# Fewer adjacency pieces per slot and fewer small VectorE operations in the first step of a graph layer

## The chip, the core and the metric

The kernel runs on one core of a Trainium2 chip. The metric is the device time of one execution in microseconds (us). The engines are called as in the profile: PE (TensorE, matrix products), DVE (VectorE), ACT (ScalarE), POOL (GpSimd) and SP (SyncE, which here only issues DMAs). [...]

## What is computed

A graph layer over N = 3327 nodes with 256 features, in two steps. In each step every node attends to all others, but only the largest probabilities that together reach 0.9 are kept. Beside it, features diffuse over a sparse adjacency matrix (about 0.12% of its entries are nonzero, and the diagonal).

```python
h = relu(layernorm(x))
R = adj + eye(N);  R = R / R.sum(-1, keepdims=True)
Z = 0;  Xf = Xa = h
for n in range(2):
    logits = (Xa @ W1.T @ W2.T) @ (Xa @ W3.T).T
    A = softmax(logits), only the top-p part (p = 0.9) kept, rows scaled to sum 1
    Xf = R @ Xf
    Xa = A @ Xa
    Z = Z + Xf @ U1[n].T + Xa @ U2[n].T
out = x + layernorm(h + Z) * g + b
```

## The kernel before

The nodes are cut into NT = 26 tiles of P = 128 rows (NP = 3328). The step loop runs over `step` 0 and 1, and inside it `i` from -1 to 27; one pass of the inner loop is called a slot here. In slot i of step 0 work on several tiles is interleaved, each piece of work being a Python generator that is advanced one stage at a time:

- `weights` (L582) makes the exponentials `e` of tile i+3. `project` (L516) makes the queries and, from `mq`, the statistics `ms` of a row's logits.
- `measured_once` (L635) guesses a row's threshold for tile i+1: two passes of ACT over the row (`through`, L633) and small operations on columns of `g`, on ACT, POOL and DVE.
- `settle` (L725) settles the exact threshold of tile i. Its stages on DVE: a pass over the row that keeps what is below the guess (`w`, L731) and `need` (L732); 20 MAX8 over segments (L736); five rounds of MAX8 and MATCH_REPLACE8 on the candidates; a running sum; the mask pass over `e` (L765); `cum` (L767) and its maximum (L769), which goes to `rec`. The final proof `prove` (L773) reads `rec`.
- `Sums` (L797) transposes the masked `e` on PE (`pt`, L810), copies it back on ACT (`eT`, L812), and multiplies with the features (`pa`, L824).
- `listed` (L837) reads the adjacency matrix. For a tile it takes 128 rows in pieces, one DMA and one DVE reduction (L846) each, and turns the block maxima into a list of the nonzero places in every row. The first nine tiles (`HALVES`) have two pieces of 13 blocks, the others seven pieces of four blocks (the last of two), in two buffers. At the end of a tile come about eight short DVE operations (L849 to L857): `lists`, four direct indices (`index`, L855) and `over`, the number of further entries.
- `packed` (L862) and `gathered` (L875) pack the further entries of a tile by small matmuls (`pb`, `po`), and `gathered` then issues the indirect DMAs on POOL: rows of the adjacency (`ac`, L894) and of the products (`xg`, L903). `diffuse` multiplies them (`pr`, L911), two slots later, in `spread`.
- `products` (L982) makes the products with U1 in the warm-up.

The order on the engines is written out by hand. `PLAN[0]` has seven strings for the seven parts of a slot of step 0; each letter advances one generator: m `measured`, d `settle`, s `spread`, a `listed`, e `first_end`, w and q `weights`, p `packed`, g `gathered`. After the seven parts the letters of a last string run what is left. The text's order is kept on PE, ACT and DVE in both steps; POOL's queue in step 0 and SP's are ordered by the scheduler.

```python
PLAN = (("mdsssa", "mdsssa", "edawwp", "msda", "mpdea", "gdawwq", "emdgq"),
c=work["d"],
a=lister if step == 0 and i else none,
for c in "lcnwqsepgb" if step else "dmwqsepgb":
```

So six pieces are read in a slot, none in slot 0. Thirteen advances of `listed` stand before slot -1, in the warm-up.

Of the kernel before, what the change touches and what calls it, by code (L numbers as in the profile page):

```python
# [9 lines left out]
F32 = mybir.dt.float32  # L10
# [3 lines left out]
AF = mybir.ActivationFunctionType  # L14
ALU = mybir.AluOpType
# [3 lines left out]
P = 128  # L19
N = 3327  # L20
D = 256
DA = 64
NT = (N + P - 1) // P
NP = NT * P
# [320 lines left out]
def guess_graph_layer(ctx, tc, x, adj, w1t, w2t, w3t, u1t, u2t, ln_g, ln_b, out, flag):  # L345
# [89 lines left out]
    back = const.tile([P, NT], F32, tag="back", name="back")  # L435
    G.iota(back, pattern=[[-1, NT]], base=NONE, channel_multiplier=-NT, allow_small_or_imprecise_dtypes=True)
    lists = const.tile([P, NT, LIST + 1], F32, tag="lists", name="lists")
    ends = const.tile([P, NT], F32, tag="ends", name="ends")
    over = const.tile([P, NT], F32, tag="over", name="over")
    index = const.tile([P, NT, DIRECT + 1], I32, tag="index", name="index")  # L440
    ax = dram.tile([NT, P, D], F32, tag="ax", name="ax")
# [74 lines left out]
    def project(step, t, queries=True, law=True):  # L516

        qp = query_at(t)
        pq = ps_t.tile([P, 4, P], F32, tag="pt", name="pq")
        pm = pq[:, 1:3, :].rearrange("p a b -> p (a b)")[:, : 2 * DA + 2]  # L520
        qT = ms = None
        if queries:
            PE.matmul(pq[:, 0, :], w2d[qp, :], query_of(t), start=True, stop=True)
        if law:
            PE.matmul(pm, query_of(t), qm[qp, step, :], start=True, stop=True)
        if queries:
            qT = tpool.tile([P, P], F32, tag="qT", name="qT", bufs=3)
            S.copy(qT, pq[:, 0, :])  # L528
        if not law:
            return qT, ms  # L530
        mq = small.tile([P, 2 * DA + 2], F32, tag="mq", name="mq", bufs=2)
        S.copy(mq, pm)
        yield


        ms = small.tile([P, 9], F32, tag="ms", name="ms")
        col = lambda k: ms[:, k : k + 1]
        V.tensor_copy(col(0), mq[:, DA : DA + 1])  # L538
        V.scalar_tensor_tensor(mq[:, : DA + 1], mq[:, : DA + 1], 1.0, mq[:, DA + 1 :], ALU.mult, ALU.mult,
                               accum_out=col(1))  # L540
        m = col(0)
        G.tensor_tensor(col(2), col(1), half[:, 1:2], ALU.pow)
        G.tensor_scalar(ms[:, 3:7], of_s, col(2), 1.0e-4, ALU.mult, ALU.add)
        G.tensor_scalar(col(7), col(1), 0.5, m, ALU.mult, ALU.add)
        G.tensor_scalar(col(7), col(7), 0.25, LNY - 0.25 * math.log(0.1 / N), ALU.mult, ALU.add)
        G.tensor_scalar(col(8), col(1), m, col(4), ALU.add, ALU.add)
        return qT, col


# [81 lines left out]
    def through(e, f, guess, sign, total):  # L631
        ja = scan.tile([P, NP], U8, tag="ja", name="ja")
        S.activation(ja, e, f, bias=guess, scale=sign, accum_out=total)  # L633

    def measured_once(r):  # L635
        e, ms = r["e"], r["ms"]


        col = guessed(r, small.tile([P, 17], F32, tag="g", name="g"))
        S.activation(col(4), col(2), AF.Square, bias=con(4))  # L640
        S.activation(col(11), col(4), AF.Identity, scale=ms(5), bias=ms(6))
        S.activation(col(1), col(0), AF.Exp, scale=-1.0, bias=con(5))
        G.tensor_scalar(col(7), col(9), -0.5, None, ALU.mult)
        G.tensor_scalar(col(8), col(9), 0.5 * NP, None, ALU.mult)
        G.tensor_scalar(col(12), col(9), -1.0, None, ALU.mult)
        G.tensor_scalar(col(5), col(1), OFFSET[0], None, ALU.mult)
        G.tensor_scalar(col(10), col(9), col(5), 1.0, ALU.mult, ALU.add)
        yield
        oa = small.tile([P, 3], F32, tag="oa", name="oa")
        through(e, AF.Relu, col(9), -1.0, oa[:, 0:1])  # L650
        yield
        through(e, AF.Sign, col(12), 1.0, oa[:, 1:2])
        yield
        S.activation(col(3), oa[:, 0:1], AF.Identity, scale=-1.0, bias=col(8))
        S.activation(col(4), oa[:, 1:2], AF.Relu, scale=col(7), bias=col(3))
        S.activation(col(6), col(4), AF.Ln, scale=col(1), bias=con(2))
        S.activation(col(3), col(4), AF.Square, scale=col(1), bias=con(1))
        S.activation(col(3), col(3), AF.Ln, scale=0.5, bias=col(10))
        S.activation(col(3), col(3), AF.Identity, scale=-1.0, bias=col(6))
        S.activation(col(3), col(3), AF.Exp, scale=col(11))  # L660
        yield

        V.tensor_scalar(col(5), oa[:, 1:2], 31.0 - NP, BIG, ALU.is_lt, ALU.mult)
        V.tensor_scalar(col(6), col(4), col(1), 0.35, ALU.mult, ALU.is_lt)
        V.scalar_tensor_tensor(col(5), col(6), BIG, col(5), ALU.mult, ALU.add)
        V.tensor_scalar(col(3), col(3), 1.0e20, col(9), ALU.min, ALU.mult)
        V.tensor_tensor(col(16), col(3), col(5), ALU.add)
# [57 lines left out]
    def settle(step, t, r):  # L725
# [38 lines left out]
        else:  # L764
            V.scalar_tensor_tensor(e, e, at(1), e, ALU.is_ge, ALU.mult, accum_out=ra)  # L765
        V.reciprocal(ra, ra)
        (G if step else V).tensor_tensor(cum[:, :n], dr[:, :n], b, ALU.mult)  # L767
        yield
        V.tensor_reduce(at(2), cum[:, :n], AX.X, ALU.max)  # L769

    def prove(step):  # L773
        v8, t, tn, Z = (rec[:, step, k, :] for k in range(4))
        ok = small.tile([P, NT], F32, tag="cum", name="ok", bufs=1)
        o2 = small.tile([P, NT], F32, tag="dr", name="o2", bufs=1)
        V.tensor_tensor(ok, v8, t, ALU.is_lt)
        V.tensor_tensor(o2, tn, t, ALU.is_lt)
        V.tensor_tensor(ok, ok, o2, ALU.mult)
        for a, c, op in ((tn, 0.0, ALU.is_gt), (t, 0.5 * BIG, ALU.is_lt),  # L780
                         (Z, 1.0e-30, ALU.is_gt), (Z, BIG, ALU.is_lt)):
            V.scalar_tensor_tensor(ok, a, c, ok, op, ALU.mult)
        V.tensor_scalar(ok, ok, 0.5, None, ALU.is_lt)
        n = N - (NT - 1) * P
        f = small.tile([P, 1], F32, tag="f", name="f")
        V.tensor_reduce(f, ok[:, : NT - 1], AX.X, ALU.add)
        V.tensor_tensor(fl, fl, f, ALU.add)
        V.tensor_tensor(fl[:n], fl[:n], ok[:n, NT - 1 :], ALU.add)
        if step == 0:
            V.tensor_scalar(ok, lists[:, :, LIST - 1], 0.0, None, ALU.is_gt)  # L790
            V.scalar_tensor_tensor(ok, ends, float(P), ok, ALU.is_gt, ALU.add)
            V.tensor_reduce(f, ok, AX.X, ALU.add)
            V.tensor_tensor(fl, fl, f, ALU.add)

# [42 lines left out]
    def listed():  # L837
        for t in range(NT):
# [13 lines left out]
            V.max(ls[:, :8], fm)  # L852
            V.match_replace(fm, ls[:, :8], fm, 0.0)
            V.max(ls[:, 8:LIST], fm)
            V.tensor_scalar(index[:, t, :DIRECT], ls[:, :DIRECT], -1.0, float(NONE), ALU.mult, ALU.add)  # L855
            of = small.tile([P, LIST], F32, tag="of", name="of", bufs=2)
            V.tensor_scalar(of[:, DIRECT:], ls[:, DIRECT:LIST], 0.0, None, ALU.is_gt, ALU.add,  # L857
                            accum_out=over[:, t : t + 1])
# [3 lines left out]
    def packed(t):  # L862

        assert t in done
        ls, end, ov = lists[:, t, :], ends[:, t : t + 1], over[:, t : t + 1]
        pb = ps_t.tile([P, 4, P], F32, tag="pt", name="pb")
        PE.matmul(pb[:, 0, :1], upto, ov, start=True, stop=True)
        S.copy(ls[:, LIST:], pb[:, 0, :1])
        yield
        V.tensor_tensor(end, ls[:, LIST:], ov, ALU.add)  # L870
        ohs[t] = oh = small.tile([P, P], F32, tag="oh", name="oh", bufs=2)
        V.tensor_scalar(oh, place, end, None, ALU.is_lt)
        V.scalar_tensor_tensor(oh, place, ls[:, LIST:], oh, ALU.is_ge, ALU.mult)

    def gathered(t):  # L875
# [1 line left out]
        ls, n = lists[:, t, :], LIST - DIRECT  # L877
        po = ps_t.tile([P, 4, P], F32, tag="pt", name="po")
        PE.matmul(po[:, 0, : n + 1], oh, ls[:, DIRECT:], start=True, stop=True)
        lo = small.tile([P, n + 1], F32, tag="lo", name="lo", bufs=2)  # L880
        S.copy(lo, po[:, 0, : n + 1])
        yield
        nth = small.tile([P, 1], F32, tag="nth", name="nth")
        V.tensor_scalar(nth, lo[:, n:], -1.0, part, ALU.mult, ALU.add)
        of = small.tile([P, LIST], F32, tag="of", name="of", bufs=2)
        V.scalar_tensor_tensor(of[:, :n], place[:, :n], nth, lo[:, :n], ALU.is_equal, ALU.mult, accum_out=nth)
        V.tensor_scalar(index[:, t, DIRECT:], nth, -1.0, float(NONE), ALU.mult, ALU.add)
        ac = adjp.tile([P, KT, P], F32, tag="ac", name="ac", bufs=2)
        nc.sync.dma_start(ac[:, KT - 1, :], adj[t, :, t, :])
        acs[t] = ac  # L890
# [201 lines left out]
    def refetch(t):  # L1092
# [7 lines left out]

    PLAN = (("mdsssa", "mdsssa", "edawwp", "msda", "mpdea", "gdawwq", "emdgq"),
            ("llcmss", "lnms", "lwwnfd", "lcmdsssg", "fmswqdf", "llmdf", "lmwfd"))

    LAST = {NT - 1: ("cfss", "cn", "ndd", "sss", "fddddsf", "f", "f"), NT: ("cf", "", "", "", "ff", "fv", "f"),
# [6 lines left out]
    for step in range(2):  # L1113
        sums = Sums(step, live, xw if step else x0, AHEAD[step])

        for i in range(-1, NT + 2):
# [4 lines left out]
            if step == 1 and i == -1:  # L1121
# [9 lines left out]
                s=spread(step, i - 2 + 2 * step) if valid(i - 2 + 2 * step) else none,  # L1131
                w=later.pop((step, i + 2), none),
                e=first_end(i - 2) if step == 0 and valid(i - 2) else none,
                a=lister if step == 0 and i else none,
                p=packed(i + 1) if step == 0 and i >= 0 and valid(i + 1) else none,
                g=none if not valid(i + 2 * step) else refetch(i + 2) if step else gathered(i),
                b=none, q=none, v=proof() if step and i == NT else work.get("v", none),
# [34 lines left out]
                run(work["m"])  # L1172
            if step == 0 and i == -1:
                G.memset(es[2][:, N:NP], 0.0)
            for c in "lcnwqsepgb" if step else "dmwqsepgb":
                run(work[c])
            if step == 0 and i == NT:
                moments(1, gsum)
# [52 lines left out]
```

## Time and profile before

| | |
|---|---|
| median of three runs | 1406.87 us (1405.7 to 1407.31) |
| profiled execution, device time | 1408.79 us |
| its span, first to last instruction | 1407.1 us |
| granted TensorE clock | 0.974 |
| PE busy | 1278.7 us, 91% |
| DVE busy | 1220.4 us, 87% |
| ACT busy | 1105.6 us, 79% |
| POOL busy | 989.7 us, 70% |
| first and last `need` (L732) of step 0 | 94.1 and 710.3 us |
| first `need` of step 1 | 790.8 us |
| last piece of the adjacency (L846) | 605.8 us |

Durations of single instructions are in microseconds in the timeline (start, duration) and in nanoseconds in the groups. On DVE an instruction can start a little before the end recorded for the one ahead of it, so the distance from start to start tells better what it occupies. A line of waits reads: engine, tile and line of the waiting instruction, `<-` what released it, then the sum of the idle time, how often, and the longest. A POOL instruction that is held up shows it as a longer duration, not as a wait.

### The profile page before, as it was taken

To read this page: it belongs to the slowest core of one execution; us is meant where nothing else is said; L and a number is where in the kernel's file an instruction comes from. 1 tells how busy PE (TensorE), PEld (TensorE's weight loads), DVE (VectorE), ACT (ScalarE), POOL (GpSimd) and SP (SyncE) were. 2 spreads that over 40 slices of the span, in tenths; PEclk is the share of its full clock that TensorE was granted. 3 is DMA by queue.
4 is the path that set the end of the run, shared out by engine and by line. 5 is a ranking of instruction groups with operands and counts; after the bars stand their busy time and mean duration, and the time that the engine had idled before them with its cause. 6 is when DMAs were issued, how large, how long until landed. Compare 5 with 4: busy or idle time off the path is not lost.

```text
span 1407.1 us, 22248 instructions
## 1 busy us (share of the span) xinstructions
PE 1278.7 (91%) x6495; PEld 980.9 (70%) x6495; DVE 1220.4 (87%) x3727; ACT 1105.6 (79%) x2423; POOL 989.7 (70%) x1348
## 2 busy tenths in 40 slices
PE   6898999999999999999999479999999999999885
PEld 5545777777777777778786257777777777777664
DVE  6868999999999999998863589999999999999981
ACT  5467887788778788787944689999999999999921
POOL 6214777667667677768862668888888888888832
PEclk9999999999999999999999579999999999999998
DMA  8874454544545445432331202213121221312100
GB/s 284 263 247 126 134 151 133 138 137 135 146 124 148 133 137 152 129 96 73 101 85 57 78 23 79 79 57 90 55 82 58 79 82 54 90 57 79 57 8 22
DMA packets 91203, 149.78 MB, mean 106 GB/s; under 512 B 15265, under 2 KB 58656, under 8 KB 91072
## 3 DMA queue, kind: packets, MB, share of 16 engines
q1 hardware_dynamic: 73616, 105.37, 24.0%
q0 software_dynamic: 16640, 42.69, 12.1%
q8 instruction: 54, 0.88, 0.3%
q14 instruction: 77, 0.63, 0.1%
q10 hardware_dynamic: 816, 0.20, 0.1%
HBM read 120.93 MB, written 27.28 MB: 105 GB/s over the span
## 4 chain that ended last, share of the span: by engine, by line
DVE 51%; PE 24%; ACT 17%; POOL 3%; issue 3%; DMA 1%; DVEq 0%; SPq 0%; POOLq 0%; ACTq 0%
ACT ja L633 11%; DVE e L765 10%; PE pa L824 9%; DVE cand L736 7%; DVE w L731 6%; DVE fm L846 5%; PE pl L600 4%; DVE bb L743 4%; DVE cand L745 4%; PE pt L810 3%; PE pz L988 2%; DVE x L765 2%; ACT eT L812 2%; PE pr L911 1%; ACT e L604 1%
## 5 line engine op out<-in xcount | busy, mean ns | idle before, releaser
L824 PE MATMUL pa<-xw,eT 128*128 128x256 f32 x1352 | 331.9, 387 | 6.6 <-DVE s L935 6.5
L633 ACT ACTIVATE ja<-e,g 128x3328 uint8<-128x3328 f32 x106 | 325.8, 3074 | 0.1
L824 PE MATMUL pa<-x,eT 128*128 128x256 f32 x1352 | 325.2, 382 | 0.0
L824 PEld LDWEIGHTS pa<-xw,eT 128*128 128x128 f32 x1352 | 250.2, 191 | 68.1 <-issue 27.1
L824 PEld LDWEIGHTS pa<-x,eT 128*128 128x128 f32 x1352 | 245.0, 192 | 26.3
L812 ACT COPY eT<-pt 128x512 f32<-128x512 f32 (+1 forms) x364 | 202.1, 556 | 76.6 <-PE pt L810 76.5
L736 DVE MAX8 cand<-w 128x8 f32<-128x168 f32 (+1 forms) x1040 | 251.3, 318 | 0.0
L810 PE MATMUL pt<-ident,e 128*128 128x128 f32 x1144 | 180.7, 278 | 60.6 <-DVE e L765 36.6
L894 POOL DMA_INDIRECT ac<-in_adj,index x130 | 130.7, 1005 | 128.2 <-DVE ms L538 91.2
L810 PEld LDWEIGHTS pt<-ident,e 128*128 128x128 f32 x1144 | 140.7, 144 | 107.3 <-issue 48.1
L903 POOL DMA_INDIRECT xg<-bx,index x130 | 184.8, 1421 | 41.0 <-issue 30.0
L731 DVE SCALAR_TENSOR_TENSOR w<-e,g 128x3328 f32<-128x3328 f32 x44 | 169.1, 3842 | 0.7
L903 POOL DMA_INDIRECT xg<-vx,index x130 | 131.1, 1009 | 45.6 <-issue 33.0
L765 DVE SCALAR_TENSOR_TENSOR e<-e,rec 128x3328 f32<-128x3328 f32 x40 | 156.6, 3915 | 0.7
L911 PE MATMUL pr<-xg,ac 128*128 128x257 f32 (+1 forms) x520 | 139.1, 391 | 11.5 <-DVE s L1086 11.3
L604 ACT ACTIVATE e<-pl 128x832 f32<-128x832 f32 x132 | 113.0, 859 | 36.4 <-PE pl L600 36.3
L911 PEld LDWEIGHTS pr<-xg,ac 128*128 128x128 f32 x520 | 93.9, 195 | 25.1 <-DVE s L1086 11.4
L743 DVE MAX8 bb<-cand 128x8 f32<-128x160 f32 x286 | 92.8, 325 | 6.4
L600 PE MATMUL pl<-after,qT 64*128 64x416 f32 x416 | 96.7, 559 | 0.5 <-ACT qT L528 0.5
L767 POOL TENSOR_TENSOR cum<-dr,bb 128x48 f32<-128x48 f32 x26 | 84.9, 3264 | 15.5 <-DVE rec L755 15.3
L951 POOL TENSOR_TENSOR s<-s,gam 128x256 f32<-128x256 f32 x25 | 92.5, 3701 | 3.2 <-ACT s L950 3.2
L600 PE MATMUL pl<-both,qT 64*128 64x416 f32 x416 | 90.8, 540 | 0.9 <-DVE both L1006 0.9
(259 smaller groups left out, 2210.7 us busy)
## 6 DMA issues: line engine op xcount, KB each, us to landing
at<-in_adj SPq DMA_DIRECT2D x102, 256.0 KB
cx<-ac SPq DMA_DIRECT2D x26, 384.0 KB
ac<-cx SPq DMA_DIRECT2D x26, 384.0 KB
wide<-in_adj SPq DMA_DIRECT2D x10, 832.0 KB
e<-in_adj SPq DMA_DIRECT2D x8, 832.0 KB
bx<-e SPq DMA_DIRECT2D x26, 128.5 KB
own<-bx SPq DMA_DIRECT2D x26, 128.5 KB
x<-in_x SPq DMA_DIRECT2D x13, 256.0 KB
```

The lines of the kernel that those rows point to most:

```text
L600: PE.matmul(pl[:, a, :wd], qT[p, :], keys_of(step, a).rearrange("p a b -> p (a b)")[:, c : c + wd], start=True, stop=True)
L633: S.activation(ja, e, f, bias=guess, scale=sign, accum_out=total)
L731: V.scalar_tensor_tensor(w, e, col(16), e, ALU.is_lt, ALU.mult, accum_out=d2)
L736: V.max(cand[:, 8 * s : 8 * s + 8], w[:, s * SEG : min(NP, (s + 1) * SEG)])
L743: V.max(b8, cand)
L765: V.scalar_tensor_tensor(e, e, at(1), e, ALU.is_ge, ALU.mult, accum_out=ra)
L810: PE.transpose(pt[:, j, :], e[:, (j0 + j) * P : (j0 + j + 1) * P], ident)
L812: S.copy(eT[:, :w, :], pt[:, :w, :])
L824: PE.matmul(self.pa, eT[:, c - 4 * k, :], self.xa[:, j, :], start=c == 0, stop=c == NT - 1)
L894: G.indirect_dma_start(out=ac[:, k, :], out_offset=None, in_=rows, in_offset=bass.IndirectOffsetOnAxis(ap=index[:, t, k : k + 1], axis=0), ...
L903: G.indirect_dma_start(out=xg[:, k, :w], out_offset=None, in_=rows, in_offset=bass.IndirectOffsetOnAxis(ap=index[:, t, k : k + 1], axis=0))
L911: PE.matmul(pr[:, :w], ac[:, k, :], own if k == KT - 1 else xg[:, k, :w], start=k == 0, stop=k == KT - 1)
```

## The change

In step 0 the letter a is taken out of the sixth part of `PLAN[0]`, which leaves five pieces in a slot; slot 0, which had none, takes three. The last d moves to the second part of the next slot as c. Small operations are dropped or put on another engine:

```diff
-        V.tensor_copy(col(0), mq[:, DA : DA + 1])
...
-        m = col(0)
+        minus = mq[:, 2 * DA + 1 :]
-        G.tensor_scalar(col(7), col(1), 0.5, m, ALU.mult, ALU.add)
+        G.tensor_scalar(col(7), col(1), 0.5, minus, ALU.mult, ALU.subtract)
...
-        G.tensor_scalar(col(12), col(9), -1.0, None, ALU.mult)
...
-        through(e, AF.Sign, col(12), 1.0, oa[:, 1:2])
+        through(e, AF.Sign, col(9), -1.0, oa[:, 1:2])
...
-        (G if step else V).tensor_tensor(cum[:, :n], dr[:, :n], b, ALU.mult)
-        yield
+        if step:
+            G.tensor_tensor(cum[:, :n], dr[:, :n], b, ALU.mult)
+        yield
+        if not step:
+            V.tensor_tensor(cum[:, :n], dr[:, :n], b, ALU.mult)
         V.tensor_reduce(at(2), cum[:, :n], AX.X, ALU.max)
...
-            V.tensor_scalar(index[:, t, :DIRECT], ls[:, :DIRECT], -1.0, float(NONE), ALU.mult, ALU.add)
+            G.tensor_scalar(index[:, t, :DIRECT], ls[:, :DIRECT], -1.0, float(NONE), ALU.mult, ALU.add)
...
-        V.tensor_tensor(end, ls[:, LIST:], ov, ALU.add)
-        V.tensor_scalar(oh, place, end, None, ALU.is_lt)
+        V.tensor_scalar(oh, place, ov, ls[:, LIST:], ALU.subtract, ALU.is_lt)
...
-        yield
         nth = small.tile([P, 1], F32, tag="nth", name="nth")
-        V.tensor_scalar(nth, lo[:, n:], -1.0, part, ALU.mult, ALU.add)
+        S.activation(nth, po[:, 0, n : n + 1], AF.Identity, scale=-1.0, bias=part)
+        yield
...
-        V.tensor_scalar(index[:, t, DIRECT:], nth, -1.0, float(NONE), ALU.mult, ALU.add)
+        G.tensor_scalar(index[:, t, DIRECT:], nth, -1.0, float(NONE), ALU.mult, ALU.add)
...
-    PLAN = (("mdsssa", "mdsssa", "edawwp", "msda", "mpdea", "gdawwq", "emdgq"),
+    PLAN = (("mdsssa", "mcdsssa", "edawwp", "msda", "mpdea", "gdwwq", "emgq"),
...
-                a=lister if step == 0 and i else none,
+                a=itertools.islice(lister, 9 if i else 3) if step == 0 else none,
...
-            for c in "lcnwqsepgb" if step else "dmwqsepgb":
+            for c in "lcnwqsepgb" if step else "cmwqsepgb":
```

The tile `ends` is gone; `prove` adds its two parts once, at the start of step 1. The sign of the second measuring pass turns, and with it the signs of two constants that are used with it. In the changed kernel the two index operations on POOL stand at L856 and L887, and the mask pass at L762.

More of the change, by code (lines that the diff above doesn't have):

```diff
@@ L437, in guess_graph_layer @@
     lists = const.tile([P, NT, LIST + 1], F32, tag="lists", name="lists")
-    ends = const.tile([P, NT], F32, tag="ends", name="ends")
     over = const.tile([P, NT], F32, tag="over", name="over")
@@ L537, in project @@
         col = lambda k: ms[:, k : k + 1]
-        V.tensor_copy(col(0), mq[:, DA : DA + 1])
         V.scalar_tensor_tensor(mq[:, : DA + 1], mq[:, : DA + 1], 1.0, mq[:, DA + 1 :], ALU.mult, ALU.mult,
                                accum_out=col(1))
-        m = col(0)
+        minus = mq[:, 2 * DA + 1 :]
         G.tensor_tensor(col(2), col(1), half[:, 1:2], ALU.pow)
         G.tensor_scalar(ms[:, 3:7], of_s, col(2), 1.0e-4, ALU.mult, ALU.add)
-        G.tensor_scalar(col(7), col(1), 0.5, m, ALU.mult, ALU.add)
+        G.tensor_scalar(col(7), col(1), 0.5, minus, ALU.mult, ALU.subtract)
         G.tensor_scalar(col(7), col(7), 0.25, LNY - 0.25 * math.log(0.1 / N), ALU.mult, ALU.add)
-        G.tensor_scalar(col(8), col(1), m, col(4), ALU.add, ALU.add)
+        G.tensor_scalar(col(8), col(1), minus, col(4), ALU.subtract, ALU.add)
         return qT, col
@@ L642, in measured_once @@
         S.activation(col(1), col(0), AF.Exp, scale=-1.0, bias=con(5))
-        G.tensor_scalar(col(7), col(9), -0.5, None, ALU.mult)
+        G.tensor_scalar(col(7), col(9), 0.5, None, ALU.mult)
         G.tensor_scalar(col(8), col(9), 0.5 * NP, None, ALU.mult)
-        G.tensor_scalar(col(12), col(9), -1.0, None, ALU.mult)
         G.tensor_scalar(col(5), col(1), OFFSET[0], None, ALU.mult)
@@ L661, in measured_once @@
         yield
-        V.tensor_scalar(col(5), oa[:, 1:2], 31.0 - NP, BIG, ALU.is_lt, ALU.mult)
+        V.tensor_scalar(col(5), oa[:, 1:2], NP - 31.0, BIG, ALU.is_gt, ALU.mult)
         V.tensor_scalar(col(6), col(4), col(1), 0.35, ALU.mult, ALU.is_lt)
@@ L790, in prove @@
             V.tensor_scalar(ok, lists[:, :, LIST - 1], 0.0, None, ALU.is_gt)
-            V.scalar_tensor_tensor(ok, ends, float(P), ok, ALU.is_gt, ALU.add)
+            V.tensor_tensor(o2, lists[:, :, LIST], over, ALU.add)
+            V.scalar_tensor_tensor(ok, o2, float(P), ok, ALU.is_gt, ALU.add)
             V.tensor_reduce(f, ok, AX.X, ALU.add)
@@ L864, in packed @@
         assert t in done
-        ls, end, ov = lists[:, t, :], ends[:, t : t + 1], over[:, t : t + 1]
+        ls, ov = lists[:, t, :], over[:, t : t + 1]
         pb = ps_t.tile([P, 4, P], F32, tag="pt", name="pb")
@@ L879, in gathered @@
         PE.matmul(po[:, 0, : n + 1], oh, ls[:, DIRECT:], start=True, stop=True)
-        lo = small.tile([P, n + 1], F32, tag="lo", name="lo", bufs=2)
-        S.copy(lo, po[:, 0, : n + 1])
+        lo = small.tile([P, n], F32, tag="lo", name="lo", bufs=2)
+        S.copy(lo, po[:, 0, :n])
+        nth = small.tile([P, 1], F32, tag="nth", name="nth")
+        S.activation(nth, po[:, 0, n : n + 1], AF.Identity, scale=-1.0, bias=part)
         yield
-        nth = small.tile([P, 1], F32, tag="nth", name="nth")
-        V.tensor_scalar(nth, lo[:, n:], -1.0, part, ALU.mult, ALU.add)
         of = small.tile([P, LIST], F32, tag="of", name="of", bufs=2)
-        V.scalar_tensor_tensor(of[:, :n], place[:, :n], nth, lo[:, :n], ALU.is_equal, ALU.mult, accum_out=nth)
-        V.tensor_scalar(index[:, t, DIRECT:], nth, -1.0, float(NONE), ALU.mult, ALU.add)
+        V.scalar_tensor_tensor(of[:, :n], place[:, :n], nth, lo, ALU.is_equal, ALU.mult, accum_out=nth)
+        G.tensor_scalar(index[:, t, DIRECT:], nth, -1.0, float(NONE), ALU.mult, ALU.add)
         ac = adjp.tile([P, KT, P], F32, tag="ac", name="ac", bufs=2)
```

## The prediction

> **What bounds the kernel now.** I read the engine shares first, then cut the span into stages, since a share over 1407 us mixes two steps. Only step 0 (about 94 to 790 us) is touched. Two windows of two slots each (a slot is one tile of 128 rows), first while lists are made, then after the last list piece (at 605.8 us):
>
> ```profile
> core 0: us, PE busy (x) PEld busy (x) DVE busy (x) ACT busy (x) POOL busy (x), PEclk, DMA share, GB/s
> 459.40:508.80 49.40, 47.80 (x256) 37.87 (x256) 47.60 (x155) 40.26 (x99) 34.71 (x45) 1.00 0.50 138
> 634.50:682.10 47.60, 47.60 (x257) 37.80 (x255) 41.16 (x133) 40.25 (x99) 41.07 (x45) 1.00 0.30 83
> ```
>
> TensorE is full in the second window and idles 1.6 us in the first, VectorE the other way round. The waits of 159.3 to 634.5 us (19 slots) say who holds whom:
>
> ```profile
> POOL ac L894 <- DVE ms L538: 66.6, 19, 6.4
> ...
> PE pt L810 <- DVE e L765: 17.5, 14, 2.0
> ```
>
> No VectorE wait stands in that answer: VectorE never rests, and TensorE waits 17.5 us for its masked tile (L765). From 634.5 to 705.2 the list of TensorE's waits is empty. So VectorE sets the slots with lists and TensorE those without. VectorE's slot, from `need` (L732) to `need`, with a list finished in it and without:
>
> ```profile
> 220.40 0.22 DVE L732 TENSOR_SCALAR need<-rec,d 128x1 f32<-128x1 f32 x1
> ...
> 245.56 0.21 DVE L732 TENSOR_SCALAR need<-rec,d 128x1 f32<-128x1 f32 x1
> ...
> 321.59 0.21 DVE L732 TENSOR_SCALAR need<-rec,d 128x1 f32<-128x1 f32 x1
> ...
> 345.54 0.21 DVE L732 TENSOR_SCALAR need<-rec,d 128x1 f32<-128x1 f32 x1
> ```
>
> 25.16 and 23.95 us. TensorE's own slot, where it never idles:
>
> ```profile
> 634.50 0.29 PE L879 MATMUL po<-lists,oh 128*128 128x13 f32 x2
> ...
> 657.85 0.29 PE L879 MATMUL po<-lists,oh 128*128 128x13 f32 x2
> ...
> 682.05 0.29 PE L879 MATMUL po<-lists,oh 128*128 128x13 f32 x2
> ```
>
> 23.35 and 24.20 us (tiles in COUNTED have six more matmuls), mean 23.78. That is the next floor.
>
> [...] POOL's L894 usually lasts 0.95 us and one that falls into the mask pass (L765) 4.39:
>
> ```profile
> 677.85 3.68 DVE L765 SCALAR_TENSOR_TENSOR e<-e,rec 128x3328 f32<-128x3328 f32 x1
> ...
> 677.96 4.39 POOL L894 DMA_INDIRECT ac<-in_adj,index  x1 [0.30 <-issue]
> ```
>
> [...] ops on one column still take 0.08 to 0.24 us from start to start, so dropping them is worth that.
>
> **The change part by part, per slot.** Starts of successive VectorE instructions give what each really occupies:
>
> ```profile
> 215.76 0.20 DVE L884 TENSOR_SCALAR nth<-lo,part 128x1 f32<-128x1 f32 x1
> 216.00 0.23 DVE L886 SCALAR_TENSOR_TENSOR of<-place,nth,lo 128x12 f32<-128x12 f32 x1
> 216.16 0.08 DVE L886 DVE_READ_ACCUMULATOR of<-place,nth,lo 128x1 f32 x1
> 216.27 0.15 DVE L887 TENSOR_SCALAR index<-nth 128x1 int32<-128x1 f32 x1
> 216.35 0.14 DVE L538 COPY ms<-mq 128x1 f32<-128x1 f32 x1
> 216.52 0.23 DVE L539 SCALAR_TENSOR_TENSOR mq<-mq 128x65 f32<-128x65 f32 x1
> ```
>
> - Dropped from VectorE: L884 0.24, L887 0.08, L538 0.17; `ends` (L870, 231.50 to 231.68) 0.18; sum 0.67. The direct index (L855, 227.78 to 227.90) 0.12 where a list ends.
> - One piece fewer (L846, 220.53 to 221.12): 0.59.
> - `cum` and its maximum (L767, L769) move to the next slot's second part. They took 0.44 + 0.10; behind each other they have to wait for one another, about 0.4. Bounds -0.3 to +0.1; I take nothing. Only the final proof reads them.
> - So a slot that ends a list falls from 25.16 to 25.16 - 0.59 - 0.12 - 0.67 = 23.78, another from 23.95 to 22.69. A list has seven pieces, so five of seven slots end one: mean 23.47.
> - The 119 small pieces are redistributed: none in slot 0 and six in each of 1 to 19 (four in 20) become three in slot 0, five in 1 to 23 and one in 24. Slots 21 to 23 rise from no pieces to 23.47 on VectorE, still under TensorE's 23.78. In slot 0 VectorE waits 0.25, 2.46, 1.41 and 1.64 us for `pz` or its DMA, which covers three pieces (1.8 us); the one piece taken out of the slot before it (89.00 to 89.60) pays for the first. I take 0.3 us gained in the warm-up, bounds -1 to +2.
> - ScalarE gets `nth` as an activation from PSUM (nearest row L881, 0.17; at most 0.3): it has about 20 us of work in a 23.8 us slot and `nth` is read some 7 us later. Cost nothing; without that slack 0.3 a slot.
> - POOL gets two index ops and loses L645. Like L644 to L645 (0.27 start to start) and L543 to L545 (0.35): 0.27 + 5/7 x 0.35 - 0.28 = +0.24. In its queue L887 stands ahead of the fifth row gather, the `ms` and `g` ops and later gathers. L856 waits for VectorE's list, but stands behind work that reaches it at about the time the list is done. The SP queue issues the same DMAs, one piece less per slot.
>
> Sum: 159.3 to 634.5 is 475.2 us for 19 slots. TensorE's floor is 10 x 24.20 + 9 x 23.35 = 452.2, so 23.0 can go: the 17.5 of waits [...]. I keep 1.9 us of slot 257.8 to 285.8, which is neither floor nor wait (granted clock 0.94), and 0.1 us in each of 22 slots (2.2), because slots at 23.78 on VectorE meet odd TensorE slots of 23.35; some 4 us of slack between `mq` and the next mask pass even this out. 23.0 - 1.9 - 2.2 + 0.3 = 19.2. Step 1 and the passage to it don't change. Against the profiled execution (1408.79 us, span 1407.1) this makes 1389.6; the median of the runs is 1.9 lower: **1387.7**.
>
> **Rivals.**
> - A, 0.57: TensorE's floor decides, as above. 1383 to 1392.
> - B, 0.27: [...] With POOL closer to full, VectorE's two long passes start behind a POOL op; the `w` pass at 661.73 took 4.14 instead of 3.68. If both cost 0.46 more, VectorE's mean is 24.4: (25.01 - 24.4) x 19 = 11.6, less (24.4 - 23.78) x 3 = 1.9 in slots 21 to 23: 9.7 gained, 1397. For it: step 1's passes do take 4.1. Against: those of step 0 mostly take 3.7.
> - C, 0.05: VectorE and TensorE overlap perfectly, the slow-clock stretch goes too and the warm-up gives 2 us: 25 gained, 1382.
> - D, 0.07: slower. POOL becomes the bound. Without waits its slot is already 23.93 us (L894 at 666.61 and 690.54), with the two ops 24.2. The index op is released just as pass `w` starts; [...] it loses the 1.25 us in which the gather now slips in (216.70 to 217.97): 25.4. The `g` columns then come late for ScalarE. (25.4 - 25.01) x 19 + (25.4 - 23.78) x 3 = 12: 1419. It decides once POOL needs over 25.0. Against: at 24.2, 0.4 over TensorE, the lag grows by about 9 us in 22 slots, while POOL's waits (3.5 a slot) and ScalarE's reading of the columns (L654 at 678.72, POOL done at 672.4) leave about 10.
> - E, 0.04: these cancel, within 0.2%.
>
> **How the numbers follow.** A is the likeliest, so 1387.7. Eight in ten: from 1383, leaving out half of C, to B's 1397, leaving out D and E. Faster by over 0.2% (2.8 us, about what a measurement of this kernel can tell from no change): A, B, C, 0.89; same 0.04; slower 0.07.
>
> **What would show it.** After: TensorE's waits for L762 (the old L765) nearly gone between 160 and 630 us, slots alternating near 24.2 and 23.4 to slot 23, small idle times of VectorE on `lists` and `mq`, the last piece in slot 24, and step 1 slots as before at 22.2 us. Wrong if VectorE still shows no wait and slots of 24.4 (B), if ScalarE waits for POOL's columns (D), or if slot 0 or the start of step 1 has grown.

## The result and the profile after

| | before | after |
|---|---|---|
| median of the comparison | 1406.28 us (1405.21 to 1407.31) | 1386.59 us (1383.37 to 1387.66) |
| ratio, 95% interval | | 0.9856 [0.9843, 0.9869] |
| profiled execution, its span | 1408.79, 1407.1 us | 1383.37, 1381.4 us |
| `po` (L879) of slot 2 | 159.3 us | 155.5 us |
| from there, 19 slots | 475.2 us | 455.7 us |
| the rest of the span | 772.6 us | 770.2 us |

The forecast was 1387.7 us. Of one later run, the second of less VectorE, 10 of 21 executions fell into a slower state and are left out of its median and ratio here. The profiled execution of after is the fastest of its four runs and that of before lies 2.5 us over its median, so the 25.7 us between the two spans are 6 more than the 19.7 between the medians: 3.8 lie ahead of slot 2, 19.5 in the 19 slots, 2.4 behind them.

The same two views as before, first the busy times: two slots with lists, then two later ones. In the old kernel the second window had no pieces left; now it still holds seven.

```profile
core 0: us, PE busy (x) PEld busy (x) DVE busy (x) ACT busy (x) POOL busy (x), PEclk, DMA share, GB/s
443.00:490.90 47.90, 47.81 (x255) 37.86 (x254) 44.94 (x138) 40.47 (x101) 39.25 (x48) 1.00 0.48 138
634.50:682.60 48.10, 47.53 (x254) 37.61 (x253) 45.98 (x138) 40.35 (x100) 39.83 (x43) 1.00 0.40 110
```

In the window with lists TensorE idles 0.1 us where it idled 1.6, and VectorE is busy 44.94 of 47.90 us where it was busy 47.60 of 49.40. The same view of all 19 slots, before and after:

```profile
159.30:634.50 475.20, 457.03 (x2417) 360.50 (x2417) 457.99 (x1451) 382.65 (x933) 346.53 (x427) 1.00 0.48 134
155.50:611.20 455.70, 453.93 (x2419) 359.49 (x2417) 434.90 (x1330) 385.25 (x952) 374.61 (x443) 1.00 0.47 135
```

TensorE's idle time falls from 18.2 to 1.8 us: that is 16.4 of the 19.5 us. The waits of TensorE, VectorE and POOL between 155.5 and 611.2 us, the same 19 slots:

```profile
PE pt L811 <- DVE e L762: 1.5, 4, 0.5
...
DVE fm L847 <- DMA at<-in_adj: 5.2, 10, 1.0
...
POOL ac L894 <- POOL index L887: 9.7, 19, 0.5
POOL index L887 <- DVE of L886: 8.2, 18, 0.6
```

TensorE's 17.5 us behind the mask pass have become 1.5. VectorE, which had no wait at all, now waits 5.2 us, all of it for the transfer of a piece. POOL's 66.6 us of waiting have become 17.9 in two lines. TensorE's slots from `po` to `po`:

```profile
467.48 0.29 PE L879 MATMUL po<-lists,oh 128*128 128x13 f32 x2
490.92 0.29 PE L879 MATMUL po<-lists,oh 128*128 128x13 f32 x2
...
611.16 0.29 PE L879 MATMUL po<-lists,oh 128*128 128x13 f32 x2
634.51 0.29 PE L879 MATMUL po<-lists,oh 128*128 128x13 f32 x2
659.47 0.29 PE L879 MATMUL po<-lists,oh 128*128 128x13 f32 x2
682.59 0.29 PE L879 MATMUL po<-lists,oh 128*128 128x13 f32 x2
```

23.44 and 23.35 us are TensorE's floor for a tile outside COUNTED (23.35). 24.96 is one inside COUNTED, 0.76 over its floor of 24.20: TensorE waits 0.6 us for the mask there. The last, 23.12, is as long as the same slot before (23.13). Over the 19 slots the sum stands 3.5 us above the floor of 452.2.

POOL is where the new cost went. One slot, VectorE's weight pass and what POOL does meanwhile:

```profile
473.56 3.69 DVE L728 SCALAR_TENSOR_TENSOR w<-e,g 128x3328 f32<-128x3328 f32 x1
473.58 0.19 POOL L887 TENSOR_SCALAR index<-nth 128x1 int32<-128x1 f32 x1 [0.62 <-DVE of L886]
474.28 3.83 POOL L894 DMA_INDIRECT ac<-in_adj,index  x1 [0.51 <-POOL index L887]
```

The index operation is released just as the pass starts, the gather behind it needs 0.51 us more, and so it issues inside the pass and takes 3.83 us where others take 0.95. Rival D had charged 1.25 us a slot for this gather's lost place. The groups of the page show that part of the loss only changed its place. Before:

```profile
L894 POOL DMA_INDIRECT ac<-in_adj,index x130 | 130.7, 1005 | 128.2 <-DVE ms L538 91.2
L903 POOL DMA_INDIRECT xg<-bx,index x130 | 184.8, 1421 | 41.0 <-issue 30.0
```

and after:

```profile
L894 POOL DMA_INDIRECT ac<-in_adj,index x130 | 189.7, 1459 | 44.3 <-issue 30.5
L903 POOL DMA_INDIRECT xg<-bx,index x130 | 158.0, 1216 | 39.2 <-issue 30.5
```

The row gathers (busy time and mean in ns after the bar) cost 59 us more in all and the other gathers 27 less. In the 19 slots POOL is busy 374.61 us where it was busy 346.53, 1.5 us more a slot. With its waits shortened POOL still fits into the slot, but not for nothing: the gather that is held hands its delay on. In the same slot, the queue of SyncE and the piece that comes late:

```profile
480.42 0.33 SPq L1082 DMA_DIRECT2D cx<-ac  x1
480.85 0.37 SPq L846 DMA_DIRECT2D at<-in_adj  x1
...
481.86 0.44 SPq L846 DMA_DIRECT2D at<-in_adj  x1
...
484.40 0.69 DVE L847 TENSOR_REDUCE fm<-at 128x4 f32<-128x512 f32 x1 [0.71 <-DMA at<-in_adj]
```

The gather ends at 478.11. SyncE's write of `cx` (L1082) starts 2.3 us after it, and the transfers of the next pieces stand behind that write in the queue. So it is in all 19 slots: `cx` follows the end of that gather by 1.8 to 2.9 us, and each of VectorE's ten waits for a piece is for one of the two transfers issued next. The waits of SyncE name the same releaser:

```profile
SPq L1082 <- DMA ac<-in_adj,index: 122.9, 19, 7.1
```

Before it was 81.6 us, with a gather of 0.95 us in that place. So VectorE's 5.2 us hang on the gather that the weight pass holds; no run frees that gather alone and so prices it.

### The profile page after: what moved, and what is told of

Same layout as the page of the kernel before. It is cut to its first block, busy times and chain, and to the rows that moved or that the text cites. A ratio compares the mean times of both kernels' runs of the same rounds, so it can differ in the third digit from the quotient of the medians.

```text
span 1381.4 us, 22149 instructions
## 1 busy us (share of the span) xinstructions
PE 1271.7 (92%) x6495; PEld 977.1 (71%) x6495; DVE 1207.6 (87%) x3595; ACT 1109.1 (80%) x2449; POOL 1022.8 (74%) x1374
## 4 chain that ended last, share of the span: by engine, by line
DVE 40%; PE 24%; ACT 17%; POOL 9%; DMA 4%; issue 4%; SPq 0%; POOLq 0%; DVEq 0%; ACTq 0%
ACT ja L631 11%; PE pa L825 9%; DVE e L762 9%; PE pl L598 5%; DVE cand L733 4%; DVE w L728 4%; DVE fm L847 4%; DVE bb L740 3%; DVE cand L742 3%; PE pt L811 3%; PE pz L988 3%; POOL xg L903 3%; POOL ac L894 2%; DVE x L762 2%; DMA at<-in_adj 2%
## 5 line engine op out<-in xcount | busy, mean ns | idle before, releaser
L894 POOL DMA_INDIRECT ac<-in_adj,index x130 | 189.7, 1459 | 44.3 <-issue 30.5
L903 POOL DMA_INDIRECT xg<-bx,index x130 | 158.0, 1216 | 39.2 <-issue 30.5
L903 POOL DMA_INDIRECT xg<-vx,index x130 | 130.9, 1007 | 45.6 <-issue 33.0
L762 DVE SCALAR_TENSOR_TENSOR e<-e,rec 128x3328 f32<-128x3328 f32 x40 | 153.6, 3840 | 0.6
L765 POOL TENSOR_TENSOR cum<-dr,bb 128x48 f32<-128x48 f32 x26 | 84.8, 3261 | 15.5 <-DVE rec L752 15.4
```

What stands on the lines that cost most here:

```text
L894: G.indirect_dma_start(out=ac[:, k, :], out_offset=None, in_=rows, in_offset=bass.IndirectOffsetOnAxis(ap=index[:, t, k : k + 1], axis=0), ...
L903: G.indirect_dma_start(out=xg[:, k, :w], out_offset=None, in_=rows, in_offset=bass.IndirectOffsetOnAxis(ap=index[:, t, k : k + 1], axis=0))
```

## The experiments

**One warning on all that follows.** The experiments ran in four groups, each on another chip at another time. On the chip of the second group the kernel before took 1404 to 1408 us, as in the first comparison. On the other three it took 1405.6 to 1417.8, 1417.1 to 1429.4 and 1413.9 to 1430.1, and every trace that was taken there, none of them of the kernel before, has a stall in the slots that no trace of the quiet group has (shown below). Whether the chip or the hour makes it can't be told apart, since each chip had one group. I compare only within a group, and take the sizes of the parts from the quiet one.

### The parts, on the chip where nothing disturbs them

The changed kernel again, beside the kernel before, the new distribution of the pieces alone, and the changed kernel with its index operations put back on VectorE.

> The changed kernel itself, beside the half changes. Theory 1 (the time of the halves belongs to the halves: each breaks a balance that the whole change has): 1384 to 1389 us, slots of 23.9 to 24.1 us, VectorE 93 to 96% busy in them, ScalarE's copy of the transposes waiting for TensorE 10 us at most over the 19 slots. Theory 2 (the stall of the first four experiments, where that copy starts some 3 us late once in a slot, comes with the chip or the execution, whatever the kernel): 1395 to 1415 us here, with that copy waiting 20 to 40 us over the slots, as in those four.

> The kernel before, for its profile. Theory 1: 1405 to 1408 us, its slots 25.0 us with VectorE 98 to 100% busy, no wait of ScalarE's copy of the transposes above 10 us over the 19 slots. Theory 2: 1412 to 1418 us, with that copy waiting 20 us or more over the slots and VectorE below 97% busy in them.

The pieces alone are the kernel before with two edits:

```diff
-"gdawwq", "emdgq"),
+"gdwwq", "emdgq"),
...
-                a=lister if step == 0 and i else none,
+                a=itertools.islice(lister, 9 if i else 3) if step == 0 else none,
```

> The new distribution of the pieces alone, a second time. Theory 1: 1420 us or more as in its first runs, about 35 us above the changed kernel on the same chip. Theory 2: it goes with the changed kernel; if that one stands at 1384 to 1389 us, this one stands at 1393 to 1397 us, what its VectorE work (0.6 us a slot more than the changed kernel's) says.

The index operations on VectorE are the changed kernel with

```diff
-            G.tensor_scalar(index[:, t, :DIRECT], ls[:, :DIRECT], -1.0, float(NONE), ALU.mult, ALU.add)
+            V.tensor_scalar(index[:, t, :DIRECT], ls[:, :DIRECT], -1.0, float(NONE), ALU.mult, ALU.add)
...
-        G.tensor_scalar(index[:, t, DIRECT:], nth, -1.0, float(NONE), ALU.mult, ALU.add)
+        V.tensor_scalar(index[:, t, DIRECT:], nth, -1.0, float(NONE), ALU.mult, ALU.add)
```

> The changed kernel with both index operations (L856, L887) back on VectorE: VectorE has two operations of some 0.06 to 0.08 us more in a slot, and the gathers are no longer behind a POOL operation. If TensorE is the bound and the wait of the gather for its index on POOL costs nothing: within 2 us of the changed kernel. If the order on POOL (index, gather, behind it) costs: 3 to 8 us faster. If VectorE is still the bound: 2 to 4 us slower. Theory 2: all of it covered by the spread of the chip.

Measured, with the profiled execution cut as above:

| | median us | ratio to before, 95% | to `po` of slot 2 | 19 slots | rest |
|---|---|---|---|---|---|
| before (seven runs of the group; the profile is one more run's) | 1406.6 | | 157.6 | 476.4 | 770.0 |
| pieces alone | 1395.73 | 0.9932 [0.9915, 0.9948] | 158.0 | 461.6 | 773.7 |
| changed, index on VectorE | 1391.9 | 0.9896 [0.9876, 0.9916] | 159.8 | 460.7 | 770.1 |
| changed | 1388.39 | 0.9871 [0.9855, 0.9888] | 156.0 | 460.9 | 770.9 |

The time of the pieces alone is the one that the second theory gave, 1393 to 1397 us. The changed kernel's time and the kernel before's (1405.75 us) were allowed by the first theory, but in the kernel before the copy of the transposes waits 20.8 us and VectorE is busy 96.4%, the signs that I had given to a stall. The trace of the first comparison has them too (21.3 us, 96.4%), so they don't mark one.

The pieces alone give 10.9 us of the 18.2, and in these traces nearly all of what the slots gain: 14.8 us of 15.5. Each split rests on one execution, and the slots of two executions of the changed kernel differ by 5.2 us. VectorE's waits are empty for that kernel, so I take its slot for what VectorE needs: 461.6 / 19 = 24.3 us, against 25.1 for the kernel before (476.4 / 19). TensorE's waits of the pieces alone, and below it POOL's gather, which still waits as in the kernel before:

```profile
PE pt L810 <- DVE e L765: 6.7, 11, 1.3
...
POOL ac L894 <- DVE ms L538: 52.9, 20, 5.8
```

The small operations then bring little in the slots, because TensorE's floor (23.8) is half a microsecond away. What is left of the 0.5 us is eaten by VectorE's wait for pieces. The 7.3 us between the two medians lie elsewhere: 2.0 ahead of slot 2 and 2.8 behind the 19 slots, 1.15 of them in slots 21 to 23, which the pieces now reach and where 24.3 us of VectorE are over TensorE's floor.

In the changed kernel on this chip, between 481 and 507 us, VectorE waits once for a transfer, 1.8 us, and then the mask comes 1.6 us late for TensorE; the slot of TensorE in which it does takes 25.97 us. Over the 19 slots the changed kernel has 7.5 us of such waits of VectorE here and 5.2 in the first comparison, TensorE 6.5 and 1.5 us behind the mask: most of the 5.2 us by which the two traces of the same kernel differ in the slots. All ten late pieces were issued right behind the write of `cx` here too. The pieces alone, whose row gathers take 947 ns in the mean of 96, have no such wait; but their VectorE is slower as well.

With the index operations back on VectorE the median is 3.5 us longer (the intervals overlap), which is what I had expected if VectorE were the bound; but the 19 slots take the same time (460.7 against 460.9). So it doesn't matter there which engine makes the index. It doesn't show that the held gather costs nothing: the gather is caught just as much without them, 1648 ns in the mean over 160 to 630 us against 1549, and VectorE waits as long for pieces (7.8 us against 7.5). What this kernel loses is 3.8 us ahead of slot 2. Its first `need` comes at 94.2 us as in the kernel before (93.9), against 89.2 in the changed kernel. In the chain of waits through VectorE's warm-up of this kernel stands the write of `ax` behind a copy of the products (start, duration):

```profile
78.13 0.70 DVE e L991
...
78.85 7.52 DMA ax<-e
```

The kernel before has the same pair (77.39 and 7.27 us). In the changed kernel the chain goes past that write, through a load of pieces instead:

```profile
73.31 7.63 DMA wide<-in_adj
...
80.96 1.90 DVE fm L847
```

So the index operations of the warm-up's lists are what the warm-up gained by, in this pair of kernels. That the products' copies come free earlier by it is my reading of the two chains; no run isolates it. The pieces alone, with the index on VectorE, also go past that write, and their first `need` comes at 92.2 us.

### The stall of the other chips

The first group had the halves and two kernels that leave work out, all on one chip where the kernel before spread over 12 us (median 1413.02).

> The kernel before with the new distribution of the pieces alone (five a slot, three in slot 0); all small operations stay. Theory (two floors, the slower of VectorE and TensorE sets a slot): VectorE's slot falls by 0.59 us, and by one finished list in seven, to a mean of 24.2 us, still over TensorE's 23.78. 19 slots gain (25.01 - 24.25) x 19 = 14, slots 21 to 23 lose 1.4: about 13 us less than before, 1393, with TensorE still waiting some 6 us for the masked tile. Rival (gains add up, VectorE alone counts): the pieces and the small operations share the measured 19.7 us in proportion to their VectorE time, 0.83 to 0.7 us a slot: 10.5 us here. Rival (POOL's queue is what was relieved): nothing here, since POOL's operations are those of before.

The operations alone are the changed kernel with the old strings of letters but for the c, and six pieces from slot 1 on:

```diff
-"gdwwq", "emgq"),
+"gdawwq", "emgq"),
...
-                a=itertools.islice(lister, 9 if i else 3) if step == 0 else none,
+                a=lister if step == 0 and i else none,
```

> The changed kernel with the old distribution (six pieces a slot, none in slot 0); small operations dropped or moved as in the change. Two floors: VectorE's mean is (25.16 - 0.79) in six slots of seven and (23.95 - 0.67) in one, 24.2 us; about 14 us less than before, 1392; the two parts alone together give 27, more than the 19.7 of both. Additive rival: 9.2 us here, and the sum of both alone equals 19.7. Rival of POOL (two more index operations cost): under 9.

Less TensorE: 2 of the 6 matmuls of `diffuse` skipped in step 0.

```diff
-            PE.matmul(pr[:, :w], ac[:, k, :], own if k == KT - 1 else xg[:, k, :w],
-                      start=k == 0, stop=k == KT - 1)
+            if k not in (2, 3) or w == D:
+                PE.matmul(pr[:, :w], ac[:, k, :], own if k == KT - 1 else xg[:, k, :w],
+                          start=k == 0, stop=k == KT - 1)
```

> The changed kernel without two of the six matmuls of the diffusion in step 0 (the third and fourth gathered entries are left out of the sum); 4 passes of 0.217 us, 0.87 us less for TensorE in a slot. Two floors: TensorE's mean falls to 22.9, VectorE's 23.47 takes over; slots go from 23.98 to about 23.55: 0.43 x 23 = 10 us less than the changed kernel, 1377, and VectorE's small waits vanish while TensorE waits for the masked tile again. Rival (POOL is already the bound): no gain. Rival (TensorE alone counts): 20 us.

Less VectorE: a small piece reduces 64 of its 128 columns. In the first trace one then occupies 0.32 us from start to start (467.55 to 467.87), against 0.59 in the kernel before (220.53 to 221.12).

```diff
-                V.tensor_reduce(fm[:, j0 : j0 + n], at[:, :n], AX.X, ALU.max, apply_absolute_value=True)
+                V.tensor_reduce(fm[:, j0 : j0 + n], at[:, :n] if t < HALVES else at[:, :n, : P // 2], AX.X, ALU.max, apply_absolute_value=True)
```

> The changed kernel with the reduction of the small pieces over 64 of 128 columns (entries of the other half are left out of the lists); about 0.27 us less for VectorE in each of five pieces, 1.3 us a slot. Two floors: TensorE's 23.78 stays, so only the imperfect overlap goes (23.98 to 23.8): at most 4 us less than the changed kernel, 1383 to 1386. Rival (VectorE still bounds): 1.3 x 23 = 30 us less, 1357.

I repeated three of them and added a dose of VectorE, in two more groups, neither of them on a quiet chip (before: median 1423.2 for the first two, 1422.1 for the last two).

> A second time, since the first stood on a chip where the kernel before itself spread over 12 us. Left out: 2 of the 6 matmuls of the diffusion product in every slot of the first step, 0.87 us of TensorE a slot (its floor falls from 23.78 to 22.91 us, read in the first trace). If TensorE alone sets the slots of the changed kernel (forecast of the prediction): they fall to what VectorE needs, 23.5 us, 8 to 9 us less than the changed kernel's ratio of 0.987 to the kernel before: ratio 0.979 to 0.982. If the two engines stand level and hand the slot from one to the other: 0.983 to 0.987, the slots stay near 24.0 us. If something else sets them (POOL, the transfers): 0.987.

> A second time, for the same reason. Left out: half of the columns that the five pieces of a slot reduce, some 0.9 us of VectorE a slot by the row of the piece. If TensorE sets the slots: only the slots longer than TensorE's floor shrink, 0 to 5 us, ratio 0.983 to 0.987, TensorE 100% busy in nearly every slot. If VectorE sets them still: 10 us and more, ratio under 0.980. If the stall of the first chip belongs to this kernel: ratio 0.995 or more, as in its first runs (1.0009).

> The operations dropped or moved alone, with the old six pieces a slot, a second time. On the undisturbed chip the pieces alone gave 10.9 us and the whole change 18.2. If the two parts add (one engine, VectorE, sets both kernels): 7 us, ratio 0.994 to 0.996. If they overlap, because behind VectorE stands TensorE's floor (VectorE 25.0 - 0.6 = 24.4 us a slot here, so the operations alone take 0.5 us off 19 slots and 3 us off the warm-up): 10 to 13 us, ratio 0.990 to 0.993. If the operations bring only the warm-up: 3 to 4 us, ratio 0.997 to 0.998.

The dose:

```diff
+        if step == 0:
+            for _ in range(2):
+                V.max(spare, cand)
```

> The changed kernel with two more MAX8 of 0.32 us in every slot of the first step, whose results nobody reads: VectorE has some 0.7 us more in a slot (23.5 becomes 24.2), TensorE nothing. If VectorE sets the changed kernel's slots: +0.7 over 24 slots, 15 to 18 us, ratio 0.998 to 1.0. If TensorE's floor (23.8) sets them and VectorE lies 0.3 us below it: 6 to 10 us, ratio 0.991 to 0.995. If VectorE has room beside TensorE: under 4 us, ratio 0.987 to 0.990.

| | first: median, ratio to before in the group | second |
|---|---|---|
| pieces alone | 1423.78, 1.0115 [1.0065, 1.0165] | 1395.73, 0.9932 (quiet chip, above) |
| operations alone | 1405.06, 0.9955 [0.9934, 0.9976] | 1417.46, 0.9967 [0.9949, 0.9986] |
| less TensorE | 1388.4, 0.9839 [0.9783, 0.9894] | 1398.67, 0.985 [0.9806, 0.9893] |
| less VectorE | 1411.91, 1.0009 [0.9981, 1.0038] | 1418.38, 0.9956 [0.9931, 0.998] |
| dose of VectorE | 1430.39, 1.0043 [1.0023, 1.0063] | |

All my numbers of the first group missed. Of the second tries, less TensorE (0.985) fell into its middle range and less VectorE (0.9956) into the one for a stall; the operations alone lie between two ranges, the dose outside all. The pieces alone are 28 us apart between two chips, while the kernel before moved by 6.4 between the same two: the stall comes with the chip or the hour, but how much it costs depends on the kernel. What it is like shows best in the second run of less VectorE, whose VectorE can't be the bound (busy 43.86 of 51.10 us from 463.8 to 514.9). Its waits of ScalarE, TensorE and VectorE, 155 to 630 us:

```profile
ACT eT L813 <- PE pt L811: 52.6, 32, 3.3
...
PE pq L522 <- ACT eT L813: 23.5, 19, 1.5
...
DVE mq L537 <- issue: 36.5, 19, 1.9
```

One ring, as I read it: ScalarE waits for transposes, TensorE then for ScalarE's copy of them, VectorE for `mq`, which ScalarE makes (the trace gives no releaser for it). TensorE's wait for that copy is the mark: 12.2 to 23.5 us in each of the eight traces of these chips, none in a quiet one. Releasers have to be read with care here: the eight traces hold 12,600 to 13,100 semaphore updates, the quiet ones 20,200 and more, so a third of what they are inferred from is missing. Seventeen of the 32 waits of ScalarE are of 1.9 to 3.3 us and make up 47.0 of the 52.6. Most are like this one, a group of transposes on TensorE and its copy on ScalarE:

```profile
508.77 0.60 PE L811 MATMUL pt<-ident,e 128*128 128x128 f32 x4
...
514.22 0.59 ACT L813 COPY eT<-pt 128x512 f32<-128x512 f32 x1 [3.08 <-PE pt L811]
```

The same place in a slot of the changed kernel on the quiet chip:

```profile
464.95 0.60 PE L811 MATMUL pt<-ident,e 128*128 128x128 f32 x4
...
467.19 0.60 ACT L813 COPY eT<-pt 128x512 f32<-128x512 f32 x1
```

Here the copy starts 2.24 us after the first transpose, right behind ScalarE's work before it; there it starts after 5.45 us, 3.08 of them idle, though TensorE's records are alike. The ends of matmuls are modelled, so the trace can't tell whether TensorE was late or its signal: what begins the ring stays open. The changed kernel on the quiet chip has 18 such waits in the same 475 us, of 9.6 us together.

With less VectorE and less TensorE on the same chip, the one with less TensorE is 23.5 and 19.7 us faster. It leaves out 0.87 us of TensorE a slot, 21 us over 24 slots, which would fit slots that the ring through TensorE sets. But it also loses most of the late copies (10.1 us of waits for the transposes in its second trace, against 52.6), so the gain may be the stall's. Either way, taking VectorE work out, which would have shown whether VectorE holds the changed kernel, shows nothing under the stall. For the same reason the dose is no price of VectorE: by the prediction's sums it has as much VectorE work as the operations alone (23.47 + 0.7 against 25.01 - 0.67 - 0.09, both 24.2), and on one chip they are 12.9 us apart. In their groups the operations alone, with the old distribution, come out faster than before, the pieces alone and the dose, with the new one, slower; whether the distribution or its meeting with the ring does that isn't shown. **Open**: the changed kernel itself was not run on such a chip, so its gain of 1.3 to 1.4% is shown for quiet ones alone. Nor were the operations alone run on a quiet one, so their share is known only behind the pieces; and whether VectorE or TensorE would give more if cheaper is left without a clean run.

## Why the prediction was right, step by step

- **The slots.** 19 slots should lose 23.0 - 1.9 - 2.2 = 18.9; they lost 19.5 in the profiled execution and 15.5 in the second pair. TensorE's waits for the mask went from 17.5 to 1.5 us as said (6.5 in the second pair), and slots of 23.35 and 24.20 are there. Rival A is what happened. Of the 23.0 us, 17.5 were those waits, 0.7 a wait for `both`, and 1.8 the slow-clock slot (26.04 us busy over a floor of 24.20). The other 3.0 have no one place in the trace: four transposes behind a wait for the mask take 0.63 us, the next four 0.60, so 14 restarts make up at most 0.4.
- **VectorE's new slot** was put at 23.47. The pieces' term was right: one piece at 0.59 and a list that ends in five slots of seven instead of six (1.21 / 7 = 0.17) make 0.76, and the pieces alone took VectorE from 25.1 to 24.3, 0.8 us. Without its transfer waits the changed kernel's VectorE takes (455.7 - 5.2) / 19 = 23.7 us, an upper bound of its need. So the two engines now stand level within 0.1 to 0.3 us. That is why a single late transfer is felt.
- **Where VectorE would idle.** I named `lists` and `mq`. Neither is in the waits; the idle time lies at the pieces' transfer (L847), which I had not costed. It is the step that failed outright: of SyncE's queue I said only that it issues the same transfers, one piece fewer, and not that they stand behind `cx`, which waits for a gather that I let be caught: 5.2 and 7.5 us of VectorE in the 19 slots. What they cost stayed within the 1.9 and 2.2 us that I had set aside (the slots stand 3.5 us over the floor) in the first comparison, not in the second (8.7 us).
- **The slow-clock slot**, 1.9 us kept: the 28.0 us slot has no counterpart after; in the first comparison all 19 are between 23.35 and 24.9 us, in the second pair three take 26.0 to 26.2. So this reserve was not spent on what I kept it for.
- **The warm-up**, 0.3 us with bounds -1 to +2: 3.8 in the first comparison, outside the bounds, and 1.6 in the second pair. I priced the three pieces of slot 0 and the one piece less ahead of it, not the index operations of the 18 pieces in the warm-up. The run with the index on VectorE gives back more than all of it (159.8 against 156.0, before 157.6), so these operations are what the term lacked.
- **cum and its maximum**, nothing: no wait on them appears. Behind each other they occupy 0.34 us (502.34 to 502.68; 0.33 to 0.35 in each of the 19 slots). Before, they took 0.44 + 0.10 in 11 of the slots and 0.10 + 0.10 in the other eight, 0.40 in the mean. No run isolates them.
- **POOL**, +0.24 us of work, and rival D. POOL's busy time grew by 1.5 us a slot. The term left out that the index operations are held themselves (L856: 1.62 us in the mean of 14, put at 0.35 for an operation and its gap) and that the gather behind them is caught (3.83 us instead of 0.95). D had the gather, but added its loss to a slot of 23.93 us that already had two operations held, the gather of 4.39 us that the prediction shows and L891 behind it (3.64). Between 155 and 620 us at most one operation is held per long pass of VectorE (2.7 to 4.2 us), after (40 of 40 passes) as before (32 of 38), so the L903 that the weight pass had held came off: 27 us. TensorE's slots, 3.5 us over its own floor in all 19, rule POOL out as the bound of the first comparison; the run with the index on VectorE leaves POOL's work as it is (369.6 and 367.4 us) and doesn't test it. Rival B asked for passes of about 4.1 us in the slots: the weight pass stays at 3.68 to 3.69 between 155.5 and 611.2 us, and the mask pass takes 3.70 us in the mean of 19, where it took 3.83 in the mean of 20.
- **Step 1 and the passage**: 772.6 to 770.2 with slots 21 to 23 in it (70.7 to 71.4, so 0.7 lost where 0.1 a slot was allowed for). The passage is 85.6 and 85.4 us. The 2.9 us that step 1 is shorter in this pair are not there in the second, where all behind slot 23 takes 699.4 and 699.5.

In the sum the errors cancel, and that is luck: the wait for transfers takes what the warm-up gives beyond 0.3 us and what the reserves left. The mechanism of the slots was right; that the total came within 1 us of the forecast is not evidence for the single terms. The parts that I could run show a different split than the text: I charged about 0.76 us each to the pieces and to the operations, and in the one order that was run on a quiet chip the pieces gave most of the slots' gain, since they came off first and TensorE's floor stopped the rest.

## What to carry to other kernels

When two engines alternate as the bound, the gain of a cut on the first ends at the second's floor: read that floor from a stretch where it runs alone (here 23.78 us), and take no more than the distance from every part together. When an operation is moved to a queue with slack, the queue's own sum is not the only thing to check: follow what waits for the work behind it. Here POOL stayed below the slot, but the gather that was caught (3.83 us instead of 0.95) held up SyncE's queue, and a transfer came late for the very engine that had been relieved. And run the kernel before on the chip of each experiment: here it moved by up to 17 us from one group to another, about as much as the change under study.

## What the runs showed of the hardware that I had not expected

- The same kernel differs from chip to chip (or from hour to hour): before took 1406.6 us in the median on one and 1413.0, 1423.2 and 1422.1 on three others, at a mean granted clock of 0.97 to 0.98 in all of them.
- In the second trace of less VectorE, on one of those chips, most of ScalarE's late copies start 5.1 to 5.6 us after the first record of their transposes, against 2.24 in the quiet slot shown, about once a slot; such waits make up most of 52.6 us in 475 us.
- A gather on POOL behind an index operation of POOL's own starts 0.51 us after that one ends (474.28 - 473.77), nearly every slot: 9.7 us in 19 of them.
- In 73 of the 78 long passes of VectorE between 155 and 620 us, before and after together, an operation of POOL starts 0.1 to 1.3 us into the pass. The first one takes 2.7 to 4.2 us in 72 of them (0.74 in the other): the gather L894, L903, the sum L928, L891 or the index L856 (2.98 us for one at 469.18, against 0.19 in the warm-up). One that starts within the first 0.08 us takes 0.19 us (L887) or 0.94 to 0.97 (the gathers). Which one is held changes with where the index is made, the total for POOL hardly (369.6 us busy in the 19 slots with the index on VectorE, 367.4 with it on POOL).
- A held gather is felt two queues further: in all 19 slots of the changed kernel SyncE's write of `cx` starts 1.8 to 2.9 us after the gather's end, and the ten pieces that VectorE waits for were issued behind it.
